# The bias of a graph convolution as one BF16 product, inside a four-layer graph network kernel

## The chip, the cores and the metric

The kernel runs on one core of a Trainium2 chip. The metric is the device time in microseconds of the whole program, the median of several executions. Before the change it is 3727.61 us, the median of 3 runs (3721.43 to 3730.53). The profile is of one execution with a span of 3731.3 us.

## What is computed

A graph with 3327 nodes, 256 features each, and a dense adjacency matrix goes through four layers. Each layer is added to its input, and the sum is normalized over the features. The change lies in layer 1, which is a graph convolution followed by a state-space block (Mamba):

```python
h = jax.nn.relu(adj @ x @ gcn_w + gcn_b)
mu = h.mean(-1, keepdims=True)
var = h.var(-1, keepdims=True)
h = (h - mu) * lax.rsqrt(var + EPS) * ln_g + ln_b
return _mamba(h, w_in, conv_w, conv_b, w_xp, w_dt, b_dt, A_log, D_skip, w_out)
```

`gcn_b` has 256 values. `_mamba` projects `h` to 1024 channels, takes a short causal convolution along the nodes, and runs a recurrence along the nodes with 16 states for each of 512 channels. Layer 0 is a mean over neighbours and a product, layer 2 a graph attention, layer 3 a two-step attention that keeps the largest probabilities up to a sum of 0.9.

## The kernel before, in words

The nodes are padded to 26 tiles of 128. All large products are in FP32. The adjacency matrix is stored transposed, in blocks of 128x128, and streams from HBM for each layer that uses it.

**Layer 0** (lines 158 to 185) loops over the 26 tiles. `aggregate` (line 106) loads a row of blocks in two halves and does 26 products (line 116). The result is scaled on VectorE (lines 172 to 175), transposed, multiplied with `w0` (line 179), and normalized into `F`. While it runs, the small weights of layer 1 come in on the same DMA queue, which is SyncE's: `gcn_w` (line 197), the bias `gcn_b` (line 201), and the others down to line 233.

**Layer 1** mixes two streams of work by hand. The generator `convolve` (line 254) does the graph convolution tile by tile, and a loop over groups of nodes does the recurrence (lines 530 to 570). Groups are 128, 256, 384 and then 512 nodes wide. In each group VectorE goes through 16 states: a product with a row of B (line 470), a scan (line 478) and a product with a row of C (line 547). TensorE sums the states into four PSUM buffers by products with the identity (line 553), and ScalarE makes the decays by exponentials (line 463). There are three buffers `db` for scans, so a scan's buffer comes free only when TensorE has done its four products. Where two groups meet, the sums are gated (line 487), multiplied with `w_out` (line 494) and added to the input (line 496).

In `convolve`, each tile goes through this chain. 26 products of the adjacency blocks with the features accumulate in one half of the PSUM tile `cb` (line 266). ScalarE copies the sum to SBUF (line 272), TensorE transposes it (line 280), and ScalarE copies that (line 282). Two products with `gcn_w` follow (line 284), then a product of a row of ones with the row of biases, which adds the bias to all 128 rows (line 285), and ScalarE reads the sum through a ReLU (line 287). VectorE takes the statistics (line 84, named `bnst`), GpSimd the reciprocal root (lines 251 to 296), ScalarE normalizes (line 299), and TensorE transposes for the projections (lines 308 and 359). The pool of `cb` has one buffer, so the next tile's products start when the ReLU has read it.

Calls of `pump()` step `convolve` forward between the states of the recurrence. That gives an order in which instructions are recorded. A scheduler then sorts each engine's instructions by its own estimate of when they are ready, except where `tc.keep_in_program_order` or `tc.high_priority` says otherwise. So a different estimate for one instruction can move others.

The bias and the ones share a tile with `w_dt`, the weights of a later small product (line 405):

```python
w_dt = wpool.tile([32 * (NG - 1) + DTR, P + D + P], F32, name="w_dt")
gb, one = w_dt[0:1, P:P + D], w_dt[0:1, P + D:]
```

Of the kernel before, what the change touches and what calls it, by code (L numbers as in the profile page):

```python
# [9 lines left out]
F32 = mybir.dt.float32  # L10
BF16 = mybir.dt.bfloat16
# [7 lines left out]
P = 128  # L19
D = 256  # L20
# [6 lines left out]
NG = DI // P  # L27
DS = 16
DTR = 16
# [14 lines left out]
def gnn_kernel(ctx: ExitStack, tc: tile.TileContext, n: int, a: dict, out: bass.AP):  # L44
    nc = tc.nc
# [36 lines left out]
    def stats(mv, y, order=lambda x: x):  # L82
        st = small.tile([P, 6], F32, name="bnst")
        order(nc.vector.bn_stats(st, y))
        nc.vector.bn_aggr(mv, st)
# [20 lines left out]
    def aggregate(atp, psum, it, rhs, cols, jh=JH, source=None):  # L106

        acc = psum.tile([P, cols], F32, name="acc")
        for j0 in range(0, nt, jh):
            m = min(jh, nt - j0)  # L110
            if source is not None:
                nc.sync.dma_start(rhs[:, j0:j0 + m, :D], source[:, j0:j0 + m, :])
            at = atp.tile([P, jh, P], F32, name="at")
            nc.sync.dma_start(at[:, :m, :], a["adjT"][it][:, j0:j0 + m, :])
            for j in range(m):
                nc.tensor.matmul(acc, at[:, j, :], rhs[:, j0 + j, :],  # L116
                                 start=(j0 + j == 0), stop=(j0 + j == nt - 1))
        return acc
# [35 lines left out]
    with tc.tile_pool(name="l1b", bufs=1) as wpool, tc.tile_pool(name="l1at", bufs=2) as l1at:  # L154
# [3 lines left out]
        with tc.tile_pool(name="l0", bufs=1) as pool, tc.tile_pool(name="l0w", bufs=2) as work, \  # L158
# [4 lines left out]
            for it in range(nt):  # L163
                if it:
                    acc = aggregate(atp, psum, it, xa, D + 1)
                else:
                    acc = aggregate(atp, psum, it, xa, D + 1, J0, a["x"])
# [10 lines left out]
                for k in range(4):  # L178
                    nc.tensor.matmul(po, xt[:, k, :] if k < 2 else mt[:, k - 2, :], w0[:, k, :],
                                     start=(k == 0), stop=(k == 3))  # L180
# [7 lines left out]
        with tc.tile_pool(name="l1aw", bufs=1) as cwork, tc.tile_pool(name="l1c", bufs=2) as ch, \  # L188
# [7 lines left out]

            gw = load(wpool, "gcn_w")

            w_dt = wpool.tile([32 * (NG - 1) + DTR, P + D + P], F32, name="w_dt")
            gb, one = w_dt[0:1, P:P + D], w_dt[0:1, P + D:]  # L200
            nc.sync.dma_start(gb, bass.AP(tensor=a["gcn_b"].tensor, offset=a["gcn_b"].offset, ap=[[0, 1], [1, D]]))
            nc.vector.memset(one, 1.0)

            def by_channel(name):
                t = wpool.tile([P, D // P], F32, name=name)
# [43 lines left out]
            def power(rs, var):  # L249

                nc.gpsimd.tensor_scalar(rs, var, EPS, None, op0=ALU.add)
                nc.gpsimd.tensor_tensor(rs, rs, mhalf[:, :var.shape[1]], op=ALU.pow)

            def convolve():

                rest = []
                full = 0
                for it in range(nt):
                    cb = cpsum.tile([P, 2, D], F32, name="cb")
                    acc, tp = cb[:, 0, :], cb[:, 1, :]  # L260
                    for j in range(nt):
                        if j % JC == 0:
                            m = min(JC, nt - j)
                            at = l1at.tile([P, JC, P], F32, name="at")
                            nc.sync.dma_start(at[:, :m, :], a["adjT"][it][:, j:j + m, :])
                        nc.tensor.matmul(acc, at[:, j % JC, :], X0[:, j, :], start=(j == 0), stop=(j == nt - 1))  # L266
                        if j % JC == JC - 1:
                            if rest:
                                rest.pop(0)()
                            yield full  # L270
                    m = cwork.tile([P, D], F32, name="m")
                    nc.scalar.copy(m, acc)
                    if rest:
                        rest.pop(0)()
                    yield full
                    if rest:
                        rest.pop(0)()
                        full += 1
                    for k in range(2):
                        nc.tensor.transpose(tp[:, k * P:(k + 1) * P], m[:, k * P:(k + 1) * P], ident)  # L280
                    mt = cwork.tile([P, D], F32, name="m")
                    nc.scalar.copy(mt, tp)
                    for k in range(2):
                        nc.tensor.matmul(acc, mt[:, k * P:(k + 1) * P], gw[:, k, :], start=(k == 0), stop=False)
                    nc.tensor.matmul(acc, one, gb, start=False, stop=True)
                    h = cwork.tile([P, D], F32, name="hn")
                    nc.scalar.activation(h, acc, AF.Relu)  # L287

                    rs = small.tile([P, 1], F32, name="rs")
                    nb = small.tile([P, 1], F32, name="nb")  # L290

                    def measure(h=h, rs=rs, nb=nb):
                        mv = small.tile([P, 2], F32, name="mv")
                        stats(mv, h)
                        power(rs, mv[:, 1:2])
                        nc.gpsimd.tensor_scalar(nb, mv[:, 0:1], rs, -1.0, op0=ALU.mult, op1=ALU.mult)

                    def norm(h=h, rs=rs, nb=nb):
                        tc.keep_in_program_order(nc.scalar.activation(h, h, AF.Identity, scale=rs, bias=nb))

                    def turn(it=it, h=h):
                        c = next(x for x in range(nch) if it * P < ends[x])
                        i = it * P - starts[c]
                        if i == 0:
                            hTs[c] = ch.tile([P, D // P, WC], F32, name="hT")
                        pt = psum.tile([P, WC], F32, name="ps")
                        for k in range(2):
                            nc.tensor.transpose(pt[:, k * P:(k + 1) * P], h[:, k * P:(k + 1) * P], ident)
                        for k in range(2):
                            nc.scalar.activation(hTs[c][:, k, i:i + P], pt[:, k * P:(k + 1) * P], AF.Identity,  # L310
                                                 scale=g1[:, k:k + 1], bias=b1[:, k:k + 1])
                    rest = [measure, lambda: None, norm, turn]
                    while it == 0 and rest:
                        rest.pop(0)()
                    full += it == 0
                    yield full
                for step in rest:
                    step()
                    full += step is turn
                    yield full  # L320

            stream = convolve()
            done = 0
            ready, valued = 0, 0
# [205 lines left out]
            for c in range(nch):  # L530
                w = us[c].shape[2]
                for s in range(DS):
# [4 lines left out]
                    k = c * DS + s + 2  # L537
# [53 lines left out]
    with tc.tile_pool(name="l3", bufs=1) as pool, tc.tile_pool(name="l3d", bufs=1, space=DRAM) as dram:  # L591
# [90 lines left out]
        with tc.tile_pool(name="l2c", bufs=1) as cpool:  # L682
# [5 lines left out]
            with tc.tile_pool(name="l2a", bufs=1) as wpool, \  # L688
# [10 lines left out]
                one = wpool.tile([2, 1], F32, name="one")  # L699
# [449 lines left out]
        with tc.tile_pool(name="l3w", bufs=2) as work, tc.tile_pool(name="l3s", bufs=4) as sm, \  # L1149
# [11 lines left out]
            with tc.tile_pool(name="l3p", bufs=2, space=PSUM) as psum:  # L1161
                es, searches, xfs, todo = {}, {}, [], None
                for i in range(-1, nt):
                    parts = []
# [229 lines left out]
```

## Time and profile before

| stretch, us | TensorE busy | VectorE busy | ScalarE busy | granted TensorE clock |
|---|---|---|---|---|
| whole span, 3731.3 | 3418.9 (92%) | 2581.8 (69%) | 1699.4 (46%) | 0.96 |
| 1260 to 1500 | 180.49 | 231.15 | 128.05 | 0.86 |
| 1500 to 3731 | 2085.35 | 1505.82 | 1064.11 | 0.98 |

Layer 0 ends at about 354 us. The first bias product starts at 369.0 us and the last at 1252.4 us. The recurrence ends at about 1570 us, layers 2 and 3 follow. Busy time of TensorE includes the time in which a pass drains while the next one streams, so a high share alone does not make it the bound. An FP32 product shows as two records of a weight load (PEld) and two of a pass (PE). In the timeline, a row gives start, busy time, engine, line, operation, output and inputs, shapes and the number of instructions merged; what stands in brackets is the idle time of the engine before it and who ended it.

### The profile page before, as it was taken

The numbers are of one execution on the slowest core, as the hardware profiler recorded it, in microseconds if no ns is written. First come the engines' busy times: TensorE is split into PE (matmuls) and PEld (weight loads), VectorE is DVE, ScalarE is ACT, GpSimd is POOL, SyncE is SP. The second block draws the span as 40 slices with busy tenths as digits, with TensorE's granted clock in tenths as the row PEclk, the third lists the DMA queues.
The fourth block names the chain that finished last, engine by engine and source line by source line (L and its number), as shares of the span: only waits on it lengthen the run. The fifth ranks groups of instructions, "written<-read, shape, count | busy, mean of one in ns | idle before, by whom it ended". The sixth has DMA issues, their size and how long they took to land. (4 is left out here: it accounts for less than half of the span.)

```text
span 3731.3 us, 41342 instructions
## 1 busy us (share of the span) xinstructions
PE 3418.9 (92%) x14823; PEld 2538.2 (68%) x14823; DVE 2581.8 (69%) x5213; ACT 1699.4 (46%) x2716; POOL 560.9 (15%) x850
## 2 busy tenths in 40 slices
PE   9999998889888877699989999999999999999985
PEld 7888876555454433378867787787777677777764
DVE  1111588999999999877754444445451899999996
ACT  1000655644445564211122333333333888888883
POOL 0000012320211100011110000000000233333332
PEclk9999999989999888899989999999999999999998
DMA  7443343333333121144422221121112222222210
GB/s 243 138 139 98 104 110 97 94 82 94 88 89 88 51 56 47 39 154 145 145 92 86 61 61 53 57 64 51 56 46 62 78 57 65 66 66 66 65 39 7
DMA packets 151985, 307.87 MB, mean 83 GB/s; under 512 B 19858, under 2 KB 73266, under 8 KB 151634
## 3 DMA queue, kind: packets, MB, share of 16 engines
q1 hardware_dynamic: 151762, 305.06, 27.5%
q8 instruction: 120, 1.97, 0.2%
q14 instruction: 103, 0.84, 0.1%
HBM read 294.36 MB, written 10.65 MB: 82 GB/s over the span
## 5 line engine op out<-in xcount | busy, mean ns | idle before, releaser
L553 PE MATMUL y<-db,ident 128*128 128x512 f32 (+3 forms) x1024 | 439.9, 572 | 63.1 <-DVE db L547 63.1
L478 DVE TENSOR_TENSOR_SCAN db<-dA,db 128x2052 f32<-128x2052 f32 (+3 forms) x128 | 463.7, 3623 | 0.9
L553 PEld LDWEIGHTS y<-db,ident 128*128 128x128 f32 x1024 | 200.0, 210 | 255.5 <-issue 157.5
L870 PE MATMUL acc<-G,wt 128*128 128x256 f32 x1352 | 338.3, 394 | 18.3 <-ACT wt L801 17.8
L870 PE MATMUL acc<-X,wt 128*128 128x256 f32 x1352 | 343.6, 391 | 9.0 <-ACT wt L868 8.6
L837 PE MATMUL acc<-F,at 128*128 128x256 f32 x1352 | 348.0, 385 | 1.1 <-ACT q L611 0.6
L266 PE MATMUL cb<-F,at 128*128 128x256 f32 x1352 | 314.1, 386 | 2.0 <-ACT hn L287 2.0
L116 PE MATMUL acc<-xa,at 128*128 128x257 f32 x1352 | 308.3, 381 | 5.7 <-DMA at<-in_adjT 5.7
L870 PEld LDWEIGHTS acc<-X,wt 128*128 128x128 f32 x1352 | 242.5, 189 | 103.9 <-issue 41.3
L837 PE MATMUL acc<-X,at 128*128 128x256 f32 x1352 | 307.9, 381 | 0.6 <-DMA at<-in_adjT 0.6
L746 PE MATMUL acc<-F,at 128*128 128x257 f32 x1352 | 303.8, 381 | 0.8 <-ACT r L719 0.8
L870 PEld LDWEIGHTS acc<-G,wt 128*128 128x128 f32 x1352 | 250.9, 193 | 78.6 <-ACT wt L801 48.5
L266 PEld LDWEIGHTS cb<-F,at 128*128 128x128 f32 x1352 | 260.4, 194 | 60.9 <-issue 16.3
L882 DVE MAX8 cand<-e 128x8 f32<-128x128 f32 x676 | 142.2, 278 | 228.3 <-ACT e L823 216.8
L463 ACT ACTIVATE dA<-dt,A_log 128x512 f32<-128x512 f32 (+3 forms) x512 | 292.1, 633 | 4.1 <-DVE dt L420 3.9
L837 PEld LDWEIGHTS acc<-F,at 128*128 128x128 f32 x1352 | 238.5, 190 | 73.9 <-issue 46.6
L116 PEld LDWEIGHTS acc<-xa,at 128*128 128x128 f32 x1352 | 255.1, 190 | 42.9 <-issue 6.4
L837 PEld LDWEIGHTS acc<-X,at 128*128 128x128 f32 x1352 | 253.0, 191 | 41.1 <-issue 8.5
L746 PEld LDWEIGHTS acc<-F,at 128*128 128x128 f32 x1352 | 253.5, 190 | 36.5 <-issue 1.0
L470 DVE TENSOR_TENSOR db<-du,row 128x2052 f32<-128x2052 f32 (+3 forms) x128 | 240.9, 1882 | 47.7 <-PE y L553 37.9
L547 DVE TENSOR_TENSOR db<-db,row 128x2048 f32<-128x2048 f32 (+3 forms) x128 | 241.2, 1885 | 26.6 <-ACT carry L481 26.6
L868 ACT COPY wt<-tp 128x512 f32<-128x512 f32 (+1 forms) x182 | 93.5, 557 | 307.8 <-PE tp L866 307.6
(302 smaller groups left out, 5207.3 us busy)
## 6 DMA issues: line engine op xcount, KB each, us to landing
at<-in_adjT SPq DMA_DIRECT2D x102, 832.0 KB, 4.5
at<-in_adjT SPq DMA_DIRECT2D x260, 320.0 KB, 3.0
row<-bc SPq DMA_DIRECT2D x80, 512.0 KB, 4.8
at<-in_adjT SPq DMA_DIRECT2D x52, 576.0 KB, 4.5
at<-in_adjT SPq DMA_DIRECT2D x26, 512.0 KB, 3.6
row<-bc SPq DMA_DIRECT2D x16, 384.0 KB, 4.9
row<-bc SPq DMA_DIRECT2D x16, 256.0 KB, 5.3
xt<-in_xT SPq DMA_DIRECT2D x26, 128.0 KB, 4.1
```

What stands on the lines that cost most here:

```text
L116: nc.tensor.matmul(acc, at[:, j, :], rhs[:, j0 + j, :], start=(j0 + j == 0), stop=(j0 + j == nt - 1))
L266: nc.tensor.matmul(acc, at[:, j % JC, :], X0[:, j, :], start=(j == 0), stop=(j == nt - 1))
L463: nc.scalar.activation(dA[:, g, 1:], dt[:, g, :], AF.Exp, scale=A[:, g, s:s + 1])
L470: tc.keep_in_program_order(nc.vector.tensor_mul(by_group(dbs[(x[0] * DS + s) % 3], w), du, B[:, 0:1, :].to_broadcast([P, NG, 1 + w])))
L478: nc.vector.tensor_tensor_scan(h[:, :m], dAs[s % 2][:, :m], h[:, :m], initial=0.0, op0=ALU.mult, op1=ALU.add)
L547: nc.vector.tensor_mul(h, h, rows.pop(0)[:, 1:2, 1:].to_broadcast([P, NG, w]))
L553: nc.tensor.matmul(ys[g][:, :w], ident, h[:, g, :], start=False, stop=(s == DS - 1))
L746: nc.tensor.matmul(acc, at[:, j, :], F[:, j0 + j, :], start=(j0 + j == 0), stop=(j0 + j == nt - 1))
L837: nc.tensor.matmul(acc, at[:, j, :], rhs[:, j0 + j, :], start=(j0 + j == 0), stop=(j0 + j == nt - 1))
L868: copy(wt[:, :m, :], pt[:, :m, :])
L870: nc.tensor.matmul(acc, wt[:, j, :], rhs[:, j0 + j, :], start=(j0 + j == 0), stop=(j0 + j == nt - 1))
L882: nc.vector.max(cand[:, s * 8:(s + 1) * 8], z[:, s * SEG:(s + 1) * SEG])
```

## The change

The FP32 product of one row of ones with one row of biases becomes a BF16 product of three rows of ones with three rows of biases. The three rows are the bias rounded to BF16, the remainder of that rounded to BF16, and the remainder of both. A BF16 number has 8 bits of significand and an FP32 number 24, so the three parts sum to the bias exactly[...]. The purpose is to take fewer passes through the array for the bias of each of the 26 tiles.

The parts are made once, on VectorE, on one partition. [...]three small copies by DMA, from SBUF to SBUF, then put the parts on partitions 0 to 2.

```diff
-            w_dt = wpool.tile([32 * (NG - 1) + DTR, P + D + P], F32, name="w_dt")
-            gb, one = w_dt[0:1, P:P + D], w_dt[0:1, P + D:]
+            w_dt = wpool.tile([32 * (NG - 1) + DTR, P + D], F32, name="w_dt")
+            gb = w_dt[0:1, P:]
             nc.sync.dma_start(gb, bass.AP(tensor=a["gcn_b"].tensor, offset=a["gcn_b"].offset, ap=[[0, 1], [1, D]]))
-            nc.vector.memset(one, 1.0)
+
+            parts = wpool.tile([1, 3, D], BF16, name="parts")
+            for k in range(3):
+                nc.vector.tensor_copy(parts[:, k, :], gb)
+                nc.vector.tensor_sub(gb, gb, parts[:, k, :])
+            bias = wpool.tile([3, D], BF16, name="bias")
+            for k in range(3):
+                nc.sync.dma_start(bias[k:k + 1, :], parts[:, k, :])
+            three = wpool.tile([3, P], BF16, name="three")
+            nc.vector.memset(three, 1.0)
...
-                    nc.tensor.matmul(acc, one, gb, start=False, stop=True)
+                    nc.tensor.matmul(acc, three, bias, start=False, stop=True)
```

Lines after the edit move down by nine, so line 285 becomes line 294 in the kernel after.

## The prediction

> **What bounds the kernel now.** I read the page first, then busy time by stretch, then the line of the bias product, and last what VectorE waits for. The slices of the page show that the limit changes with the stage, so the totals (TensorE 92%, VectorE 69%) decide nothing here. The stretches, in the order span, TensorE product, weight load, VectorE, ScalarE, GpSimd, clock, DMA share, GB/s:
>
> ```profile
> 0.00:354.00 354.00, 347.86 (x1613) 300.26 (x1614) 63.46 (x219) 23.22 (x62) 1.01 (x7) 1.00 0.49 158
> 354.00:560.00 206.00, 194.91 (x926) 158.91 (x925) 131.38 (x165) 123.09 (x321) 25.40 (x37) 0.96 0.40 105
> 560.00:1260.00 700.00, 610.34 (x1951) 372.00 (x1950) 649.95 (x365) 360.97 (x683) 133.74 (x83) 0.92 0.32 88
> ```
>
> Layer 0 (to 354) is TensorE's: 347.86 of 354 us. From 354 to about 560 TensorE still leads (95%, against 64% for VectorE), and the state-space scan starts up beside the convolution. From 560 to 1260 VectorE leads (93%), and TensorE, at 87% of modelled busy time and a clock of 0.92, has pauses. The bias product belongs to the last two stretches only:
>
> ```profile
> L285 PEld LDWEIGHTS cb<-w_dt x52: 181/184/333, 369.0 to 1252.5; 1*128 1x128 f32 x52
> L285 PE MATMUL cb<-w_dt x52: 374/478/791, 369.0 to 1252.7; 1*128 1x256 f32 x52
> ```
>
> There are 26 such products, one a tile, and each shows as two loads and two passes. The start times of TensorE's timeline tell what one takes from the stream:
>
> ```profile
> 410.69 1.13 PE L284 MATMUL cb<-gcn_w,m 128*128 128x256 f32 x4
> 411.75 0.69 PE L285 MATMUL cb<-w_dt 1*128 1x256 f32 x2
> 412.37 0.49 PE L359 MATMUL ps<-hT,w_in 128*128 128x128 f32 x2
> ```
>
> A steady row, L266 x46 in 10.14 us from 356.37, has a pass every (10.14 - 0.38) / 45 = 0.217 us, with its loads hidden. Four weight passes should so take 0.87 us, but the bias begins 1.06 us after them: its first load, 0.19 us, is bare. Its own slot is 0.62 us, two passes of 0.217 and the second load, bare again. So a bias takes 0.62 + 0.19 = 0.81 us of TensorE. At eight tiles (627, 779, 824, 866, 1000, 1042, 1175 and 1216 us) its two records span 1.22 us in place of 0.69, at a lower clock. What VectorE waits for in the convolution's two stretches (first 360 to 480, then 560 to 1260):
>
> ```profile
> DVE db L470 <- PE y L553: 19.6, 7, 6.0
> ...
> DVE db L547 <- ACT carry L481: 16.8, 25, 3.3
> DVE db L470 <- PE y L553: 12.6, 7, 4.4
> DVE u L379 <- ACT u L374: 11.7, 9, 1.9
> DVE sz L487 <- PE y L553: 4.2, 1, 4.2
> DVE bnst L84 <- ACT hn L287: 2.8, 3, 1.5
> ```
>
> Early, VectorE waits for TensorE to free a scan buffer: time won on TensorE then moves the scan. Later its idle time is 49 us in 700, in small pieces, and only 2.8 us stand right behind the chain of bias, ReLU and statistics.
>
> **What the Trainium skill says.** "FP8 and Floating Point Precision", section TensorE Precision Notes: true FP32 is four passes through the array, and BF16 is taken natively. The trace shows two records for a product, each about twice one 256-column stream, which agrees. "TensorE: Matmul & The Clock Gate", section Back-to-back issue gap: a warm pass takes N/2.4 + 2.5 ns, 109 ns for 256 columns, half of the 217 ns seen for an FP32 pass. Its section LDWEIGHTS prices a load by columns and not rows, at 128/1.2 = 107 ns, and Weight-path perf modes says that 128 non-FP32 weights load about twice as fast. The 1-row FP32 load in the trace takes 184 ns, as the 128-row one does (190), so rows indeed don't count; no run shows a BF16 load. The same page, section The HAM clock gate: the array falls to half rate after idle time; the records at 0.79 us beside those of 0.38 agree.
>
> **The change, part by part.**
> The 26 FP32 products go, and 26 BF16 ones come, each with one load. Removed: 0.81 us. Added, as an estimate from the page's figures: a stream of 0.11 us; its load bare, 0.05 to 0.11; and, since 0.11 us hides only part of the next FP32 load of 0.19, another 0.08 to 0.19 bare. That is 0.24 to 0.41 us; I take 0.31, so 0.5 us is saved a tile (0.4 to 0.57). Were the stream as slow as one FP32 pass, with both loads bare, it would be 0.19 + 0.22 + 0.19 = 0.60, a saving of 0.2: the low end.
>
> On the path, first stretch: nine tiles start their bias by 563 us. In the first two, TensorE itself waits for the ReLU (0.47 us at 370.20 and 391.86), as the next tile accumulates in the same PSUM buffer; in the next seven it runs nearly without a gap. 9 x 0.5 = 4.5 us, all of it passed on to the scan by the waits of 19.6 us.
>
> Second stretch: 17 tiles, mostly hidden under VectorE. Where VectorE stands behind the chain (the three bnst waits, 1.49, 0.73 and 0.58 us) I take 0.5 each, 1.5 us; of the seven buffer waits I take three as standing behind a bias, another 1.5 us.
>
> The order of the built program moves as well, since its scheduler believes that the ReLU comes sooner. TensorE keeps its order through the first eight tiles but for the bias, later single products change places. VectorE gets the statistics of a tile one place earlier at three points that matter. One is in the first full-width group:
>
> ```profile
> 776.68 2.28 DVE L547 TENSOR_TENSOR db<-db,row 128x2048 f32<-128x2048 f32 x1
> 778.89 4.42 DVE L478 TENSOR_TENSOR_SCAN db<-dA,db 128x2052 f32<-128x2052 f32 x1
> 783.23 0.40 DVE L84 BATCH_NORM_STATS2 bnst<-hn 128x6 f32<-128x256 f32 x1
> ```
>
> There the statistics now stand before the scan of 4.42 us. The ReLU they need ends at 780.73 + 0.38 = 781.1; at the low clock the bias gives back about 1.0, so the scan, and on it all later scans, waits from 778.9 to 780.1: +1.2. Likewise at 629.19 the statistics come before a product with the row: ReLU ready at 630.45 - 0.5, +0.8. The third, at 476.6, waited 0.5 anyway: 0. Together +2.0. The first residual additions move ahead of a scan too; their products end at 914.9 us and they would start at 915.4, so they cost nothing. ScalarE gets the ReLU before an exponential, a copy or a skip product at about 16 tiles. Its waits there (14.4 us in 12) may grow, but it idles 255 us waiting for scans in these stretches: 0.
>
> The parts: three copies and three subtractions on one partition. No row has that shape; the 1x128 memset took 0.165 us and a 128x256 addition (L182) 0.42, so 1.0 to 2.5 us, say 2. The bias lands at 31.39 + 3.2 = 34.6 us. Four of the operations fit VectorE's wait of 2.37 us for TensorE before 36.94; the last two stand before that tile's statistics and delay a row of the layer's output by 0.9 us, first read at 354. VectorE is busy 63 of 354 us there: 0.
>
> Three 512-byte copies from SBUF to SBUF are new on the DMA queue, and the last waits for the third VectorE copy, at about 37.7 us. Behind it in the queue stand the small weights of layer 1 and the next adjacency block. That block was issued at 41.28 only because its buffer was held till then; copies, two small loads and w_in are through by about 40: 0. The landing, 3 to 4 us as for the other small loads, is some 320 us ahead of the first use. The memset of ones only changes its shape, and the smaller w_dt tile frees bytes: 0. Layers 2 and 3 keep their order.
>
> Sum: -4.5 - 1.5 - 1.5 + 2.0 = -5.5 us, 3727.6 - 5.5 = 3722.
>
> **The rivals.**
> *Most of it counts.* If TensorE's stream sets the pace through the second stretch too, since scan, projections and residuals all queue on it: 18 warm tiles at 0.55 = 10, and eight at the low clock at about 1.0 = 8, so 18 us and 3710. For it: the clock is low and VectorE's waits for u and y sum to 28 us. Against it: VectorE is 93% busy there, and TensorE pauses up to 5.9 us.
> *The new order costs more.* ReLU ahead of other work in the queue of ScalarE: if each of 16 moves makes the exponentials wait one operation more (0.66 us for 128x512) and the scans feel it, 10.6 us, plus 2.0 on VectorE, with the gain lost in it: 3740, slower. For it: ScalarE did wait up to 2.24 us at the ReLU. Against it: the exponentials are done one scan ahead.
> *Nothing arrives.* The early 4.5 us is met again by VectorE's own work once it becomes the bound before 560, and the stalls of 2.0 take the rest: 3727. For it: VectorE is 85% busy from 480 on.
>
> **How the numbers follow.** My forecast has 0.55, the wash 0.16, most of it counts 0.18, the costly order 0.11. Predicted is 3722. A saving of 0.2 a tile in the early stretch would give 3725, one of 0.57 with half of the hidden ones 3717. The three runs of before spread over 9 us. The range of 3711 to 3733 leaves out the best of the first rival and the worst of the second. The bound of 0.3% is 11.2 us, 3716.4 to 3738.8. The forecast and the wash lie inside. Faster 0.19, same 0.71, slower 0.10.
>
> **What would show it.** The bias line should have 26 passes and 26 loads, and the start of the weight passes to the start of what follows the bias should fall from 1.68 us to about 1.2. Layer 0 should still end at 354, and the ninth bias (562.7) come 4 to 5 us sooner. A VectorE wait for the ReLU of about 1 us should appear before the scan near 779, and the last bias (1252.4) come some 5 us sooner, with the end shifted alike. Wrong it would be if a switch between number formats costs the array something no record here shows, if the early gain is gone by 600, or if ScalarE's waits at the ReLU rise well above 14.4 us and the scans wait for the exponentials.

## The result, and the profile after

| | median, us | ratio to before, 95% interval |
|---|---|---|
| before | 3729.07 (3721.43 to 3733.05) | |
| after | 3712.27 (3709.67 to 3716.73) | 0.9959 [0.9939, 0.9979] |
| after, second series (e3_after_again below) | 3711.25 (3707.71 to 3715.34) | 0.9948 [0.9935, 0.9960] |

The kernel after is faster by 17 us by the medians (16.8 and, in its second series, 17.1), by 15 to 19 us by the two ratios: three times the 5.5 us of the forecast. The time lies 1.3 us inside the lower end of the range, and beyond the bound of 3716.4 us that the forecast took for "faster".

Busy time by stretch in the profile after, in the columns of before:

```profile
0.00:354.00 354.00, 346.21 (x1599) 297.72 (x1600) 64.40 (x222) 23.02 (x61) 1.02 (x7) 1.00 0.48 158
354.00:560.00 206.00, 191.74 (x942) 156.94 (x940) 133.13 (x168) 125.86 (x331) 26.03 (x37) 0.99 0.36 106
560.00:1260.00 700.00, 612.31 (x1972) 374.48 (x1972) 664.00 (x382) 363.88 (x687) 194.21 (x84) 0.93 0.31 89
```

The third stretch has moved: VectorE does 664.00 us of work in the same 700 us in place of 649.95, so its idle time fell from 50 to 36 us. TensorE's busy time there did not fall (612.31 for 610.34), because work of later tiles has come into the stretch. VectorE itself does the same work in the whole span, 2582.4 us for 2581.8. What was won is idle time of VectorE.

The groups of the bias product:

```profile
L294 PEld LDWEIGHTS <-three x26: 90/91/102, 372.0 to 1236.1; 3*128 3x128 bf16 x26
L294 PE MATMUL cb<-bias,three x26: 277/278/392, 372.0 to 1236.1; 3*128 3x256 bf16 x26
```

Its first appearance between full streams on TensorE's timeline: before, the row that follows those shown in the forecast; after; and with no bias at all (e8 below):

```profile
412.70 0.61 PE L553 MATMUL y<-db,ident 128*128 128x128 f32 x4
```

```profile
410.29 1.13 PE L293 MATMUL cb<-gcn_w,m 128*128 128x256 f32 x4
411.36 0.28 PE L294 MATMUL cb<-bias,three 3*128 3x256 bf16 x1
411.56 0.49 PE L368 MATMUL ps<-hT,w_in 128*128 128x128 f32 x2
411.89 0.61 PE L562 MATMUL y<-db,ident 128*128 128x128 f32 x4
```

```profile
410.83 1.13 PE L321 MATMUL cb<-gcn_w,m 128*128 128x256 f32 x4
411.80 0.38 PE L395 MATMUL ps<-hT,w_in 128*128 128x128 f32 x2
412.02 0.61 PE L589 MATMUL y<-db,ident 128*128 128x128 f32 x4
```

There are 26 passes and 26 loads where there were 52 of each. The slot from the bias to what follows is 0.20 us; it was 0.62. A tile so saves 0.41 us at the full clock, from 1.68 to 1.27 us. The bias still begins 1.07 us after the weight products, as before (1.06), although its load takes 0.09 us and not 0.18. But without a bias what follows begins 0.97 us after them, so only 0.10 us of the gap belongs to the bias. Another 0.10 lies behind it: the next product takes 0.49 us, and 0.38 without a bias. From the weight products to the row of `y` it is 2.01 us before, 1.60 after and 1.19 without a bias. So a bias took 0.82 us of TensorE and takes 0.41 now.

The wait of VectorE for the scan buffers from 360 to 480 us, and then its waits from 560 to 1260 us:

```profile
DVE db L479 <- PE y L562: 16.2, 6, 6.0
```

```profile
DVE db L556 <- ACT carry L490: 14.4, 23, 2.6
DVE u L388 <- ACT u L383: 9.5, 7, 1.6
DVE db L479 <- PE y L562: 6.0, 4, 2.1
DVE sz L496 <- PE y L562: 5.8, 3, 5.0
DVE bnst L84 <- ACT hn L296: 0.9, 3, 0.3
```

The early wait of 16.2 us is no gain: it was 19.6 in the first trace of before, but 16.2 in the second (e11 below). In the later stretch the buffer wait (L470 before, L479 now) halved, from 12.6 to 6.0 us. The waits for the carry, for u and for the ReLU fell as well, by 2.4, 2.2 and 1.9 us. Only the gate (`sz`) waits longer, by 1.6.

The point of the forecast near 779 us, where the statistics now stand ahead of a scan, on VectorE's timeline after:

```profile
772.56 2.28 DVE L556 TENSOR_TENSOR db<-db,row 128x2048 f32<-128x2048 f32 x1
774.77 0.43 DVE L84 BATCH_NORM_STATS2 bnst<-hn 128x6 f32<-128x256 f32 x1
775.11 4.42 DVE L487 TENSOR_TENSOR_SCAN db<-dA,db 128x2052 f32<-128x2052 f32 x1
```

The stall of 1.2 us is not there: the statistics start as the product ends, and cost the scan nothing but their own time, which they would have taken later.

### The profile page after: what moved, and what is told of

Its sections match the earlier page's. It is cut to its first block, busy times and chain, and to the rows that moved or that the text cites. A ratio compares the mean times of both kernels' runs of the same rounds, so it can differ in the third digit from the quotient of the medians.

```text
span 3708.2 us, 41298 instructions
## 1 busy us (share of the span) xinstructions
PE 3402.6 (92%) x14797; PEld 2532.1 (68%) x14797; DVE 2582.4 (70%) x5219; ACT 1698.3 (46%) x2716; POOL 616.2 (17%) x850
## 5 line engine op out<-in xcount | busy, mean ns | idle before, releaser
L879 PE MATMUL acc<-G,wt 128*128 128x256 f32 x1352 | 337.6, 393 | 17.9 <-ACT wt L810 17.4
L275 PE MATMUL cb<-F,at 128*128 128x256 f32 x1352 | 306.6, 379 | 2.8 <-ACT hn L296 2.8
L275 PEld LDWEIGHTS cb<-F,at 128*128 128x128 f32 x1352 | 254.9, 190 | 57.6 <-issue 16.8
L479 DVE TENSOR_TENSOR db<-du,row 128x2052 f32<-128x2052 f32 (+3 forms) x128 | 240.6, 1880 | 34.7 <-PE y L562 27.3
## 6 DMA issues: line engine op xcount, KB each, us to landing
xt<-in_xT SPq DMA_DIRECT2D x26, 128.0 KB, 3.9
```

The source lines that it names most:

```text
L479: tc.keep_in_program_order(nc.vector.tensor_mul(by_group(dbs[(x[0] * DS + s) % 3], w), du, B[:, 0:1, :].to_broadcast([P, NG, 1 + w])))
L879: nc.tensor.matmul(acc, wt[:, j, :], rhs[:, j0 + j, :], start=(j0 + j == 0), stop=(j0 + j == nt - 1))
```

## How the experiments are measured

Beside the timed runs I use layer 1 in each trace: from the first product of a block with `F` on TensorE to the reduction with which VectorE begins layer 2. I split it at the first gate, the product of `y` and `sz` that closes the first group, for a reason that the first trace below gives. "Weights to next" is the time from the start of the weight products to the start of what follows the bias, summed over the 26 tiles. Each trace is of one execution. Each ratio is to runs of the kernel before in the same series, whose medians go from 3726.32 to 3730.48 us, so kernels of different series are compared by their ratios and not by their medians.

| kernel | median, us | ratio, 95% interval | layer 1 | to the first gate | after it | weights to next |
|---|---|---|---|---|---|---|
| before | 3729.07 | | 1235.9 | 128.2 | 1107.7 | 58.5 |
| e11_before_again | 3730.45 | 0.9999 [0.9989, 1.0008] | 1233.4 | 125.9 | 1107.5 | 57.3 |
| after | 3712.27 | 0.9959 [0.9939, 0.9979] | 1213.8 | 123.1 | 1090.7 | 43.9 |
| e3_after_again | 3711.25 | 0.9948 [0.9935, 0.9960] | 1213.1 | 123.1 | 1090.0 | 42.9 |
| e1_bf16_old_order | 3714.23 | 0.9962 [0.9949, 0.9975] | 1225.7 | 125.3 | 1100.4 | 46.4 |
| e12_old_order_again | 3716.71 | 0.9964 [0.9952, 0.9977] | 1223.3 | 123.0 | 1100.3 | 44.5 |
| e2_fp32_new_order | 3725.70 | 0.9990 [0.9982, 0.9998] | 1228.9 | 125.7 | 1103.2 | 57.8 |
| e5_vector_old | 3712.24 | 0.9962 [0.9948, 0.9976] | 1218.1 | 123.9 | 1094.2 | |
| e6_scalar_old | 3714.41 | 0.9968 [0.9957, 0.9980] | 1221.0 | 126.2 | 1094.8 | |
| e4_bf16_first | 3716.05 | 0.9965 [0.9952, 0.9977] | 1219.9 | 125.0 | 1094.9 | 38.7 |
| e7_first_new_order | 3715.30 | 0.9969 [0.9957, 0.9981] | 1214.2 | 126.4 | 1087.8 | 36.7 |
| e8_no_bias | 3715.56 | 0.9966 [0.9955, 0.9978] | 1214.8 | 127.5 | 1087.3 | 37.0 |
| e9_three_products | 3722.46 | 0.9981 [0.9973, 0.9989] | 1233.4 | 128.0 | 1105.4 | 54.4 |
| e10_fp32_first | 3723.06 | 0.9981 [0.9975, 0.9988] | 1226.6 | 128.4 | 1098.2 | |

In e4, e7 and e10 the bias stands first, with other work between it and the weight products, and "weights to next" does not count it (left out for e10); e8 has no bias. In e9 the sum misses the bias of one tile, 0.4 us. So the figures of these rows are no saving on the 43.9 and 42.9 of the kernel after. For e5 and e6 the sum is not needed.

## Experiment: the kernel before, once more

The kernel is unchanged.

> The kernel before once more, for a second trace of it. If the length of layer 1 (1235.9 us in the first trace) and the lower clock in its second tile (36 passes in 11.02 us, 8.05 us in the kernel after) belong to the kernel, layer 1 takes 1234 to 1238 us and these passes about 11 us again. If they were chance of one execution, either may differ by up to 3 us.

The second tile's run of 36 passes on TensorE's timeline, in the first trace of before, in the second, and after:

```profile
391.86 11.02 PE L266 MATMUL cb<-F,at 128*128 128x256 f32 x36 [0.47 <-ACT hn L287]
```

```profile
391.12 8.06 PE L266 MATMUL cb<-F,at 128*128 128x256 f32 x36 [0.47 <-ACT hn L287]
```

```profile
393.55 8.06 PE L275 MATMUL cb<-F,at 128*128 128x256 f32 x36 [0.87 <-ACT hn L296]
```

The same instructions took 11.02 us in one execution and 8.06 in another. The slower clock in this place was the chance of one execution and no property of the kernel. Of all 14 traces, nine show 8.05 to 8.34 us here and five 9.74 to 11.02. It makes up the 2.3 us between the two first gates; after the first gate, layer 1 takes 1107.7 and 1107.5 us. So I compare the part after the first gate, which repeats to 0.7 us (1090.7 and 1090.0, 1100.4 and 1100.3 as well), and take e11 as the reference for the part ahead of it: 125.9 to 123.1, or 2.8 us, are the change's there at most, as TensorE's granted clock in this part was 0.99 in e11 and 1.00 after. Layer 1 as a whole is shorter by 1233.4 - 1213.4 = 20 us.

## Experiments: the shorter product alone, the new order alone

In layer 1 three things differ between the kernels: TensorE's work, the delay of the ReLU, and the order of the instructions on each engine. The first pair splits off the order. Edges without a semaphore tell the scheduler that one instruction of an engine comes after another, so that each engine has the order of the other kernel, but for the bias product itself and its parts:

```diff
+PINS = ((1761, 1781), (1792, 1761), ...)
...
+            for later, earlier in PINS:
+                tc.add_manual_dep(nc.find_inst_by_name(f"I-{later}"), f"I-{earlier}", mybir.DependencyInfo(
+                    mybir.DependencyClass.NoSync, mybir.DependencyReason.DATA), reason="order")
```

The BF16 bias in the order of before:

> The BF16 bias, with every engine's instructions of layer 1 held in the order of the kernel before (ordering edges without a wait). If the gain is TensorE time and the latency from bias to ReLU, this keeps most of it: ratio to before 0.995 to 0.997. If the gain is mostly that residual additions and statistics stand earlier on VectorE in the new order, it keeps less than half: 0.998 to 1.000.

The FP32 bias in the order of after:

> The FP32 bias, with every engine's instructions of layer 1 held in the order of the kernel after. If TensorE time is the cause: 0.999 to 1.002, since an early ReLU on ScalarE then waits longer. If the order is the cause: 0.996 to 0.998.

The whole change once more, beside them on the same chip:

> The kernel after, unchanged, on the same chip as the two halves of it: 0.995 to 0.997 under both theories. The two halves should sum to it if they act independently.

By the ratios, the shorter product alone brings 14 us and the order alone 3.7 (0.7 to 6.7 by its interval); the two together 15 to 19. By layer 1 after the first gate it is 7.2 and 4.4 us, and together 17.2. The 4.4 rests on one trace, whose granted clock after the gate was 0.92, for 0.91 in both traces of before; how much of it is the clock is not known. The trace of e1 and its times differ by more than I liked, so it ran again:

> The BF16 bias with every engine in the order of the kernel before, a second time, since its first trace and its first times disagree: layer 1 was 10.3 us shorter than in the first trace of the kernel before (7.8 than in the second), the time 14.2 us. If the trace is the better measure of what the slot alone brings, the ratio is 0.997 to 0.998 and layer 1 takes 1223 to 1227 us again. If the times are, and the order adds little to the slot, the ratio is 0.9955 to 0.9965.

The ratio was 0.9964, so the times repeat (12.5 us), and so does layer 1 after the first gate. With 2.9 us ahead of the gate, layer 1 is shorter by 10.1 us in e12. The remaining 2 us between trace and times lie inside the interval of the ratio, 8.6 to 17.9 us. What is safe: the shorter product alone makes most of the gain, the order a smaller part, and by the traces the two together bring about 5 us more than their sum. By the times alone that surplus can't be told from none.

What each part takes away is seen in one full-width group. I took the waits of VectorE from the fourth gate to the fifth, in all four kernels. Before (175.32 us, of which VectorE is busy 164.72):

```profile
DVE db L547 <- ACT carry L481: 4.3, 5, 3.3
DVE db L470 <- PE y L553: 2.4, 2, 1.7
DVE u L379 <- ACT u L374: 2.3, 2, 1.5
DVE bnst L84 <- ACT hn L287: 1.5, 1, 1.5
```

The shorter product in the old order, e12 (171.66 us, busy 164.61):

```profile
DVE db L595 <- ACT carry L529: 4.3, 5, 3.3
DVE u L427 <- ACT u L422: 2.3, 2, 1.5
DVE bnst L123 <- ACT hn L335: 0.3, 1, 0.3
```

The FP32 product in the new order, e2 (173.73 us, busy 164.66):

```profile
DVE db L590 <- ACT carry L524: 2.9, 5, 1.8
DVE db L513 <- PE y L596: 1.9, 1, 1.9
DVE db L513 <- ACT dA L506: 1.8, 1, 1.8
DVE u L422 <- ACT u L417: 1.5, 1, 1.5
DVE bnst L127 <- ACT hn L330: 0.7, 1, 0.7
```

After (170.70 us, busy 164.45):

```profile
DVE db L556 <- ACT carry L490: 2.9, 5, 1.8
DVE u L388 <- ACT u L383: 1.5, 1, 1.5
DVE db L479 <- PE y L562: 1.3, 1, 1.3
DVE bnst L84 <- ACT hn L296: 0.3, 1, 0.3
```

The four tables read like a two-by-two plan. The shorter product takes away the waits for buffers (2.4 us) and most of that for the ReLU (1.5 to 0.3 us; in the second traces 0.7 and 0.9), and leaves the other two as they are. The new order takes 1.4 us from the wait for the carry and 0.8 from that for u. As I read the timelines, it does so because a residual addition now stands ahead of a scan: in the kernel after, the statistics of the group end 30.0 us and not 35.6 us after the gate, and ScalarE's normalization of that tile begins at 41.2 us in place of 43.8. It stands ahead of a carry copy in ScalarE's queue.

In e2 one wait is new: 1.8 us of the product with the row of B. The list names the decays `dA`, but the code of that product writes a `db` buffer and reads `du` and a row; it does not read `dA`. The buffer is the thing to look at. TensorE's and VectorE's timelines there:

```profile
992.22 1.22 PE L328 MATMUL cb<-w_dt 1*128 1x256 f32 x2
993.37 6.68 PE L596 MATMUL y<-db,ident 128*128 128x512 f32 x8
...
1000.14 2.30 DVE L513 TENSOR_TENSOR db<-du,row 128x2052 f32<-128x2052 f32 x1 [1.83 <-ACT dA L506]
```

The same place in the profile after:

```profile
989.52 0.39 PE L294 MATMUL cb<-bias,three 3*128 3x256 bf16 x1
989.84 5.32 PE L562 MATMUL y<-db,ident 128*128 128x512 f32 x8
...
995.54 2.26 DVE L479 TENSOR_TENSOR db<-du,row 128x2052 f32<-128x2052 f32 x1
```

The products that free the buffers stand behind the bias. In e2 they end at 993.37 + 6.68 = 1000.05 us, and VectorE goes on at 1000.14. In the kernel after they end at 995.16, just before VectorE needs the buffer. So the new order makes VectorE early, and the FP32 bias then makes it wait; the shorter bias takes that wait away. This is one place of about 1.8 us in a group, read from the trace and not tested by itself.

The surplus is not made in this group: alone the two parts bring 3.7 and 1.6 us there, together 4.6. It lies behind the fifth gate. From the fifth to the sixth it is 174.7 us before, 172.8 in e12, 174.4 in e2 and 170.7 after; from the sixth to the seventh 169.8, 169.7, 171.3 and 168.3. In the latter VectorE waits 1.3 us for the products of residual additions in e12 and e2, 1.2 us for `du` before and in e2, and for neither in the kernel after. Why is not shown.

## Experiments: which engine's order

The kernel after, with the order of before on VectorE alone, and then on ScalarE alone (same edges, one engine's list each):

> The kernel after with VectorE's instructions of layer 1 held in the order of before, all other engines in the new order. In the traces layer 1, from its first product to the end, takes 1235.9 us before, 1225.7 with BF16 in the old order, 1228.9 with FP32 in the new order and 1213.1 with both. If the new order acts through VectorE (residual additions and statistics ahead of a scan), this gives about 1222 to 1226; if through ScalarE, 1213 to 1216.

> The kernel after with ScalarE's instructions of layer 1 held in the order of before, the other engines in the new order. If the new order acts through ScalarE (the ReLU ahead of exponentials and copies), layer 1 takes 1220 to 1226 us; if through VectorE, 1213 to 1216.

As a whole, layer 1 in e6 lies in the range for ScalarE (1221.0 us), and in e5 between the two ranges (1218.1). After the first gate, it is longer than in the kernel after by 3.5 us with VectorE's old order (1094.2 for 1090.7) and by 4.1 with ScalarE's (1094.8). What VectorE waits for from 560 to 1260 us in e6 shows the second:

```profile
DVE u L423 <- ACT u L418: 13.3, 10, 1.6
...
DVE bnst L119 <- ACT hn L331: 3.9, 6, 1.6
```

In the kernel after these two are 9.5 and 0.9 us. So by this trace putting the ReLU earlier in ScalarE's queue was a gain for VectorE, and no cost. The times agree in sign at most: the ratios of 0.9962 and 0.9968 lie too near to 0.9959 and 0.9948 for their intervals to say so.

## Experiments: is there more to gain

The BF16 bias as the first product of its sum, so that it can run while ScalarE still copies the transposed tile; once with the order that the scheduler gives it, and once with the rest in the order of after:

```diff
+                    nc.tensor.matmul(acc, three, bias, start=True, stop=False)
                     for k in range(2):
-                        nc.tensor.matmul(acc, mt[:, k * P:(k + 1) * P], gw[:, k, :], start=(k == 0), stop=False)
-                    nc.tensor.matmul(acc, three, bias, start=False, stop=True)
+                        nc.tensor.matmul(acc, mt[:, k * P:(k + 1) * P], gw[:, k, :], start=False, stop=(k == 1))
```

> The BF16 bias as the first product of its sum (start of the accumulation), before the two weight products, while ScalarE still copies their operand. If the time from the last product to the ReLU and the bare weight loads matter, a further 0.3 to 0.4 us a tile is won, up to 8 us: 0.993 to 0.995. If the order matters alone (nearly that of the kernel after), it equals the kernel after.

> The BF16 bias as the first product of its sum, and all other instructions held in the order of the kernel after. Its own order gave layer 1 1219.9 us although the slot of weights and bias fell by another 4.2 us over the 26 tiles. If the order spent that gain, layer 1 now takes 1208 to 1211 us, and the whole 0.993 to 0.995 of before; if TensorE's time stopped counting, 1213 to 1216.

And no bias at all, which leaves out the addition of the bias, with the rest in the order of after:

```diff
-                        nc.tensor.matmul(acc, mt[:, k * P:(k + 1) * P], gw[:, k, :], start=(k == 0), stop=False)
-                    nc.tensor.matmul(acc, three, bias, start=False, stop=True)
+                        nc.tensor.matmul(acc, mt[:, k * P:(k + 1) * P], gw[:, k, :], start=(k == 0), stop=(k == 1))
```

> The product with the bias is left out (the result lacks the bias), all else held in the order of the kernel after. It takes another 0.4 us a tile, some 10 us with the low clock, from TensorE. If TensorE's time goes through to the end as from FP32 to BF16 (10 of 12 us), layer 1 takes 1204 to 1207 us; if it has become slack, 1211 to 1214.

None beats the kernel after: the ratios are 0.9965, 0.9969 and 0.9966, for 0.9959 and 0.9948. Layer 1 in e7 lies in the range for a time that stopped counting, and in e8 just above it (1214.8 us). After the first gate e7 and e8 are 2.9 and 3.4 us shorter than the kernel after, and that is all that is left to win there. At the full clock the change took 0.41 us of a bias and left 0.41; by the traces in the new order, the first half gave 12.5 us after the gate (1103.2 to 1090.7) and the second 3.4. With no bias at all the buffer wait from 560 to 1260 us is still 3.0 us, and the carry (14.4), u (9.5) and the gate (5.8) wait as long as after. Ahead of the first gate both traces lost 3.3 and 4.4 us, most of it in the second tile, whose 36 passes took 10.76 and 10.92 us there. As e11 shows, that can be chance. The intervals of e7 and e8 overlap with those of the kernel after, so a loss is not shown either.

## Experiments: TensorE's time, or the delay of the ReLU

The BF16 parts as three products of one row each, the rest in the order of after:

```diff
-                    nc.tensor.matmul(acc, three, bias, start=False, stop=True)
+                    for k in range(3):
+                        nc.tensor.matmul(acc, three[0:1, :], parts[:, k, :], start=False, stop=(k == 2))
```

> The bias as three BF16 products of one row each, every one with its own load (no copies to other partitions), everything else in the order of the kernel after on every engine. Number format and order are those of the kernel after, but the slot on TensorE should be near that of the FP32 product again: three streams of about 0.11 us and bare loads of about 0.09 to 0.19 us, some 0.7 to 0.8 us a tile in place of 0.40. Theory 'TensorE's time in the slot is the gain': layer 1 takes 1223 to 1230 us, as with the FP32 product in this order (1228.9), and the ratio is about 0.998 to 0.999. Rival 'it is the number format or the small changes around it (tiles, copies, the moved memset), not the time': layer 1 takes 1213 to 1217 us and the ratio is 0.995 to 0.9965.

TensorE's timeline there:

```profile
410.70 0.50 PE L330 MATMUL cb<-parts,three 1*128 1x256 bf16 x3
411.13 0.49 PE L404 MATMUL ps<-hT,w_in 128*128 128x128 f32 x2
```

The slot is 0.43 us in place of 0.20, less than expected: the loads of the second and the third product are hidden. The saving on the FP32 product, whose slot is 0.62, is 0.19 us a tile, and not 0.41. The ratio went back to 0.9981. So neither the number format nor the tiles and copies around it make the gain; without the one short product, more than half of it is gone. Layer 1 in this trace (1233.4 us) came out above both expectations, and after the first gate it is only 2.1 us shorter than in e11, so by the trace nearly all of the gain is gone. The trace is that of the longest of the 18 runs, 3731.7 us for a median of 3722.5, so for the size I go by the times.

The FP32 bias as the first product, in the order of before (the edit of e4 with the FP32 operands, and the edges):

> The FP32 bias as the first product of its sum and not the last, with everything else in the order of the kernel before. TensorE does the same work in the same number of passes and loads, but the bias can run while ScalarE still copies the transposed tile, so it leaves the chain from the weight products to the ReLU. Theory 'what counts is the stream of TensorE, every product behind the bias': layer 1 takes 1231 to 1237 us, as before (1235.9), ratio 0.998 to 1.0015, less what the pauses ahead of the weight products hide. Rival 'what counts is the delay of the ReLU, which VectorE's statistics and ScalarE stand behind': layer 1 takes 1224 to 1228 us, as with the BF16 product in the order of before (1225.7), ratio 0.996 to 0.9975.

The two measures disagree: a ratio of 0.9981, near the first theory, and a layer 1 of 1226.6 us, as the second one had it. After the first gate it is 9.3 us shorter than e11. The experiment also turned out to be less clean than planned, as TensorE's timeline of it shows at many tiles:

```profile
815.98 0.69 PE L325 MATMUL cb<-w_dt 1*128 1x256 f32 x2
816.61 1.98 PE L403 MATMUL ps<-hT,w_in 128*128 128x512 f32 x4
824.19 2.07 PE L329 MATMUL cb<-gcn_w,m 128*128 128x256 f32 x4 [5.60 <-ACT m L327]
```

In its old place behind the weight products, after a pause of several us, the bias ran at the low clock and took 1.21 us in this tile (at 824.21 us before). Here it runs ahead of the pause, at the full clock, in 0.69 us, and its time comes out of the pause. So moving it shortens TensorE's stream as well as the delay of the ReLU, and the two stay unseparated. What it adds is that the place of the product is worth some 7 us by the times, with no change of its number format.

## Why the prediction was right, and where it was not

**One product, one load, 26 times:** right. The cost of the old bias, 0.81 us, was right too (0.82), though not its parts: of the 0.19 us that I put ahead of it, about 0.10 is there without a bias, and as much lies behind it instead. The estimate of 0.31 us for load, stream and next load was too low: it is 0.41. The term that was too small is the bare load behind the bias, put at 0.08 to 0.19 us: it is 0.10 in the slot and 0.10 in the next product. Ahead of the bias it is 0.10, inside the 0.05 to 0.11 I had named. The load did shrink to 0.091 us, which agrees with the factor of two in "TensorE: Matmul & The Clock Gate", section Weight-path perf modes. The stream was right: e9 has two more such passes in 0.43 - 0.20 = 0.23 us, 0.11 us each, as that page's section Back-to-back issue gap prices it. The saving is 0.41 us a tile and not 0.5, inside the bounds given.

**The first stretch:** right in mechanism and nearly in size. From the start of layer 1, the ninth bias comes after 206.32 us in e11 and after 203.04 us in the kernel after, 3.3 us sooner, as much as 8 x 0.41 (3.5 us in the second trace of after). I had named 4 to 5 us sooner at 562.7. In the traces' own time it is 559.9, since layer 0 ended 2.9 us later in the trace after. Of those, 2.0 us were there before 30 us, ahead of the first use of anything that the change added; the rest is the queue's, below.

**The second stretch:** this is the step that failed: "17 tiles, mostly hidden under VectorE", with 3.0 us for six selected places. Of the 20 us in layer 1 some 3.3 lie ahead of the ninth bias, so the second stretch gave about 16.7, where the forecast had 3.0 - 2.0 = 1.0. VectorE's 93% were true, and the conclusion false. The idle 7% are 50 us, and many small pieces of them end behind something that stands behind a bias, or changes place with the ReLU. In the full-width group, the shorter product alone took 3.7 us off the 10.6 that VectorE idled (2.4 us between the other two traces, e11 and e1). A group has four tiles, whose biases give 0.82 us each at the low clock and 0.41 at the full one: 1.6 to 3.3 us. No less arrived than TensorE saved there.

**The low clock:** I had put "about 1.0" a tile for it. It is 3.15 - 2.33 = 0.82 at the tile that starts its weight products near 1173 us before (1158 after). The records agree with the section The HAM clock gate of the same page in that TensorE is slow after a pause: in e10 four passes took 2.07 us after an idle 5.60, in place of 1.13. They also show a low clock where no pause was longer than about 1 us, and not each time (11.02 and 8.06 us for the same passes).

**The new order, +2.0 us on VectorE:** wrong in sign. The stall near 779 us was worked out with the low clock at that tile (3.15 us from weights to next). In the second trace of the kernel before it is 1.80 us there: I had built on one execution's clock. The order gained 3.7 us by the times (0.7 to 6.7) and 4.4 in one trace of layer 1 after the first gate, by my reading through the residual addition and the normalization, which I had costed at nothing.

**The parts on VectorE:** as foreseen. A cast takes 0.27 us and a subtraction 0.41, 2.0 us together.

**The queue, put at 0:** too low by about 1 us. The third copy was issued by 40.0 us, as foreseen, but loads further back came late. VectorE's products with the attention vectors of layer 2, early in layer 0, waited for one of them, before and after:

```profile
68.42 0.42 DVE L236 SCALAR_TENSOR_TENSOR t<-wg,t 128x256 f32<-128x256 f32 x1 [2.19 <-DMA t<-in_attn_dst]
```

```profile
75.76 0.42 DVE L245 SCALAR_TENSOR_TENSOR t<-wg,t 128x256 f32<-128x256 f32 x1 [3.55 <-DMA t<-in_attn_dst]
77.39 0.44 PE L101 MATMUL ps<-ident,m 128*128 128x128 f32 x2 [0.73 <-DVE m L175]
```

In the kernel after they delay the scaled sum `m` of a tile of layer 0, and TensorE waits for it; from this tile to the next it took 14.2 us in place of 13.2. All ten traces with BF16 parts have the late loads, and this tile is longer by 0 to 1.4 us in them; the four with the FP32 bias have neither. This cost lies outside of layer 1, and the times contain it.

**The rivals:** "Most of it counts" had the size, 18 us for 15 to 19. Its reason was TensorE's stream alone, at 0.55 and 1.0 us a tile; TensorE saved 11 to 14 us (57.3 in e11 less the 46.4 to 42.9 of "weights to next"), and the rest came with the new order. "The new order costs more" fell: ScalarE waited 11.0 us for the ReLU and not more than 14.4. One place in e2, with the FP32 product, shows that the new order can cost, but through a buffer that TensorE frees late and not through the exponentials. "Nothing arrives" fell with the ninth bias, whose gain is still there and larger at the last: the last bias comes 16.7 us sooner, counted from the start of layer 1 as in e11.

**The range:** that it held the result was in part luck. The mechanism of the forecast gave a third of the gain. The range reached down to 3711 us, well below the 3717 us of the forecast's own best case, and so into the first rival, which had a chance of 0.18 beside the forecast's 0.55.

What remains open is how much of the gain is TensorE's time and how much the earlier ReLU, since every edit that shortened one shortened the other.

## What to carry to other kernels

An engine that is 93% busy is not a cover under which savings elsewhere vanish: ask what its idle 7% wait for, because in a loop of engines that hand buffers to each other every one of those pauses can end behind the work that is made shorter. Such a gain also runs out: the next 0.41 us a tile gave far less here. When an edit changes a scheduler's estimate, run the new order with the old work and the old order with the new work; the two effects may help each other. Before a stall is worked out from a clock in one trace, look at the same place in a second execution.

## What was not expected of the hardware

A bias behind the weight products costs about 0.10 us ahead of its pass and 0.10 us in the product behind it, whether its load takes 0.184 us or 0.091. In e9 there is no such gap between one product of few rows and the next: two more take 0.23 us. The gap so belongs to the change between tiles of 128 rows and of few rows, or to the change to the bias as such, and not to the length of its load. The runs don't tell which.

The same 36 passes after the same pauses of 0.5 to 1 us took 8.06 us in one execution and 11.02 us in another of the same kernel.
